# A second stage whose order is written out in 112 steps a period in place of 28

## The chip, the core and the metric

The kernel runs on one core of a Trainium2 chip. A core has five engines with a queue of their own each: TensorE (PE, with its weight loads, PEld), VectorE (DVE), ScalarE (ACT), GpSimd (POOL) and SyncE (SP, which here only issues DMAs). An engine works through its queue in order, and an instruction waits on semaphores for what other engines or DMAs have to deliver first. The metric is the device time of one execution in microseconds (us), as the median of several runs.

## The reference

Two layers, each behind a layer norm and added to its input. The first is a selective scan over 16 sequences of 1024 tokens with 512 channels and 16 states. The second keeps a part of the tokens (mixture of depths): a router scores every token, the 128 best of each sequence are found, and the best 127 of them go through attention and a feed-forward block; all the others pass through. Cut to the second layer:

```python
def _L0_ffn_ref(x, attention_mask, position_ids, router_w, ..., ln1, ln2):
    weights = (x @ router_w)[..., 0] + router_b[0]
    k = int(CAP * s)                       # 128 of 1024
    topv, topi = jax.lax.top_k(weights, k)
    thr = topv[:, -1]
    sel_mask = (weights > thr[:, None]).astype(x.dtype)
    sel_idx = jnp.sort(topi[:, :kc], axis=1)          # kc = 127
    x_sel = x[bidx, sel_idx]
    m_sel = m[bidx[:, :, None], sel_idx[:, :, None], sel_idx[:, None, :]]
    hn = rmsnorm(x_sel, ln1)
    q = rope(heads(hn @ wq), pos_sel); kk = rope(heads(hn @ wk), pos_sel); v = heads(hn @ wv)
    sc = jnp.einsum('bhqd,bhkd->bhqk', q, kk) / np.sqrt(hd) + m_sel[:, None]
    a = jax.nn.softmax(sc, axis=-1)
    o = (a @ v) @ wo
    x1 = x_sel + o
    x2 = x1 + jax.nn.gelu(rmsnorm(x1, ln2) @ w1) @ w2
    out = jnp.zeros_like(x).at[bidx, sel_idx].set(x2 * w_sel[..., None])
    return out + x * (1.0 - sel_mask)[..., None]
x = x + scan_layer(_layernorm(x))
x = x + _L0_ffn_ref(_layernorm(x), ...)
```

## The kernel before, in words

Everything is float32. `build` runs two stages one after the other. `scan_layer` computes the first layer and leaves its result in one DRAM tensor per sequence (`x1_dram`); the change does not touch it. `ffn_layer` is the second stage.

`ffn_layer` is a software pipeline over the 16 sequences. Its last lines run 18 periods, p = -1 to 16. In period p five generators run side by side, each on another sequence: `feed(p-1)` (the feed-forward block), `attention(p)`, `keep_others(p)` (the tokens that pass through), `select(p+1)` (top 128, gathers, first norm) and `scores(p+2)` (router). A period is a loop over `PERIOD` = 28 values of a clock. At each value the five are resumed once in that fixed sequence. A generator goes on issuing instructions until it meets an `until(k)` with k larger than the clock, and pauses there. So the numbers in `until(...)`, and nothing else, set the order in which the instructions of the five sequences stand in the engines' queues (`tc.manual_schedule()`: nothing is reordered later). They are no times. An engine that waits for one sequence's data also holds back what the other four put behind it.

What each generator does, with the lines that are spoken of later:

- `scores(b)` (L765, with `Router.scores` from L102): eight chunks of 128 tokens, each loaded as half of a tile `x1a`; per chunk on DVE `bn_stats` (L118), `bn_aggr` (L119) and a product with the router's weights (`xw`, L120). Then variance (ACT root, L128), the scores (`w_pad`, L139), a transpose on PE (`wt_ps`, L144), a copy on ACT (`w_t`, L146), and two DMAs on SP: `w_dram` (L148) and back, spread over all partitions, as `w_row` (L150). `w_row` is what `select` of the next period compares with.
- `select(b)` (L774): for each of eight chunks the rank of every token is counted on DVE (`junk` L788 and L792, `tie` L797), all ranks are added (L802, L803), eight one-hot tiles `sel` are made (L808), a threshold is summed (L815, L816). PE picks positions, weights and indices (`sd_ps`, L822; copy on ACT L826); DVE turns them into row numbers (`at`, L830 to L836); POOL gathers the mask's rows (`m_rows`, L838) and the tokens (`x1_sel`, L842). Then the angles (L861 to L868), the mask's transposes on PE (`tp_m`, L731) and their copies (`mT`, L874), `xs` (L877), the selected mask (`ms_ps`, L883), the first norm (`rmsnormed`), sine and cosine on ACT (`trig`, L891 and L892, then DVE L894), and the transposed, weighted norm `hnT` (L742).
- `attention(b)`: products with `wq`, `wk`, `wv` (L922), rotation of q and k on DVE (L934 to L942), transposes (`tp_q`, `tp_k`), logits (`sc`, L964), softmax: scaled and masked logits `a` (L970) and maximum `mx` (L976) on DVE, exponentials on ACT (L978), reciprocal `sm` (L987) and product (L988) on DVE; transposes of the weights (`tp_a`, L994; copies `aT`, L996), `o_ps` (L1003), `at_ps` (L1011), the residual on DVE (L1015), the second norm and `h2T` (L742).
- `feed(b)`: four `up` products of four matmuls each (L1029), GELU on ACT (L1034), transposes (`tp_g`), sixteen `ff_ps` matmuls (L1054), the residual and the weight on DVE (L1059, L1062), and on POOL a scatter that adds the rows to `out` (L1063).
- `keep_others(b)`: per pair of chunks two ACT instructions in place on a tile `x1b` (L908) and a store to `out` from SP (L912).

Matmul results go to PSUM banks: tag "mm" has four (`up`, the projections, `sc`, `at_ps`), "tp" two (all transposes, `sd_ps`, `ms_ps`), and `o` and `ff` one each. The loads of `x1a` and `x1b` (L673) are issued at fixed values of the clock. A logical float32 matmul of 512 columns appears as two records in the trace, a transpose as one.

Of the kernel before, what the change touches and what calls it, by code (L numbers as in the profile page):

```python
# [625 lines left out]
def ffn_layer(  # L626
# [8 lines left out]
    nc = tc.nc  # L635
# [10 lines left out]
    UP = F // 512  # L646
    PERIOD = 28
    assert K == P and RG * ND == H and UP == 4
# [112 lines left out]
    def scores(b):  # L761
        def chunk(c):
            if c == 2:
                load(b, 6, "x1a")
            return x1_of["x1a", b, c // 2 * 2][:, c % 2, :]  # L765

        first = 9 if b == 1 else 0
        return router.scores(
            b, until, [first + c if first or c < 6 else c + 7 for c in range(NT)] + [19, 20, 22],
            chunk, lambda c: row.tile([P, D], F32, tag="tmp", name=f"xw_{b}_{c}"),  # L770
            lambda name: pst.tile([P, 512], F32, tag="tp", name=name), True,
        )

    def select(b):  # L774
# [7 lines left out]
        for c in range(NT):  # L782
            yield from until(c)
            mine = w_col[:, c : c + 1]
            lo, hi = c * P, (c + 1) * P
            junk = row.tile([P, L], mybir.dt.bfloat16, tag="junk", bufs=1, name=f"junk_{b}_{c}")
            if c:
                nc.vector.tensor_scalar(  # L788
                    junk[:, :lo], w_row[:, :lo], mine, None, ALU.is_ge, ALU.add,
                    accum_out=cnt[:, 0, c : c + 1],  # L790
                )
            nc.vector.tensor_scalar(  # L792
                junk[:, lo:], w_row[:, lo:], mine, None, ALU.is_gt, ALU.add,
                accum_out=cnt[:, 1, c : c + 1],
            )
            tie = row.tile([P, P], F32, tag="tie", bufs=1, name=f"tie_{b}_{c}")
            nc.vector.scalar_tensor_tensor(  # L797
                tie, w_row[:, lo:hi], mine, earlier, ALU.is_equal, ALU.mult,
                accum_out=cnt[:, 2, c : c + 1],
            )  # L800
# [3 lines left out]

        yield from until(8)
        sel = keep.tile([P, NT, P], F32, tag="sel", bufs=1, name=f"sel_{b}")
# [11 lines left out]

        yield from until(10)
        sd_ps = pst.tile([P, 512], F32, tag="tp", name=f"sd_ps_{b}")  # L820
        for c in range(NT):
            nc.tensor.matmul(  # L822
                sd_ps[:, :SIDE], sel[:, c, :], side[:, c, :], start=(c == 0), stop=(c == NT - 1)
            )
        sd = small.tile([P, SIDE], F32, tag="sd", name=f"sd_{b}")
        nc.scalar.copy(sd, sd_ps[:, :SIDE])  # L826
        yield from until(12)
        at_f = small.tile([P, 3], F32, tag="at_f", name=f"at_f_{b}")
# [23 lines left out]
        keeping[b] = (by, plus)  # L852
        yield from until(15)

# [14 lines left out]

        yield from until(19)  # L870
        mT = row.tile([P, NT, P], F32, tag="mT", bufs=1, name=f"mT_{b}")
        for q in range(0, NT, 4):
            tp = turned(m_rows[:, q * P : (q + 4) * P], f"m_{b}_{q}")
            nc.scalar.copy(mT[:, q : q + 4, :], tp)  # L874
        yield from until(20)
        xs = keep.tile([P, D], F32, tag="xs", bufs=3, name=f"xs_{b}")
        nc.scalar.activation(  # L877
            xs, x1_sel, AF.Identity, bias=sd[:, OFF : OFF + 1], scale=sd[:, RSTD : RSTD + 1]
        )
        yield from until(20)  # L880
        ms_ps = pst.tile([P, 512], F32, tag="tp", name=f"ms_ps_{b}")
        for c in range(NT):
            nc.tensor.matmul(  # L883
                ms_ps[:, :P], mT[:, c, :], sel[:, c, :], start=(c == 0), stop=(c == NT - 1)
            )
        yield from until(21)
# [12 lines left out]
    def keep_others(b):  # L899

        by, plus = keeping.pop(b)
        for q in range(0, NT, 2):
            yield from until(1 + q if q < 6 else 18)
# [8 lines left out]
            nc.sync.dma_start(  # L912
                out[b, q * P : (q + 2) * P, :].rearrange("(c p) d -> p c d", p=P), x1
            )

    def attention(b):
        x1_sel, xs, sd, at, ms, trig, hnT = picked.pop(b)
        def projected(name, k):
            ps = psm.tile([P, D], F32, tag="mm", name=f"{name}_ps_{b}")
            for c in range(ND):  # L920
                yield from until(k + c // 2)
# [33 lines left out]
        yield from until(8)  # L955
        kT = taken(turned(k, f"k_{b}"), f"kT_{b}", "kT")
        a_of = []
        for g in range(0, RG, 2):
            yield from until(9 + g // 2)
            sc = [psm.tile([P, ND, P], F32, tag="mm", name=f"sc_{b}_{g + i}") for i in range(2)]  # L960
            for c in range(ND):
                for i in range(2):
# [21 lines left out]
        for g in range(RG):  # L984
            a, ak, sm = a_of[g]
            yield from until(11 + g)
            nc.vector.reciprocal(sm, sm)  # L987
            nc.vector.tensor_tensor(  # L988
                ak, ak, sm.unsqueeze(2).to_broadcast([P, ND, KC]), ALU.mult
            )  # L990
            yield from until(12 + g)
            tp = pst.tile([P, ND, P], F32, tag="tp", name=f"tp_a_{b}_{g}")
# [4 lines left out]
            aT.append(t)  # L997
        yield from until(16)
        o_ps = psa.tile([P, ND, P], F32, tag="o", name=f"o_ps_{b}")
# [9 lines left out]
        for c in range(ND):  # L1009
            yield from until(17 + c // 2)  # L1010
# [3 lines left out]
        yield from until(19)  # L1014
        nc.vector.tensor_tensor(xs, xs, at_ps, ALU.add)  # L1015
        h2 = rmsnormed(xs, f"h2_{b}")
        yield from until(23)
        h2T = gained(turned(h2, f"h2_{b}"), 1, f"h2T_{b}", "qT")
        attended[b] = (x1_sel, xs, sd, at, h2T)

    def feed(b):
# [3 lines left out]
        def unit(f):  # L1025
            up = psm.tile([P, 512], F32, tag="mm", name=f"up_{b}_{f}")
            for c in range(ND):
                yield from until(2 * f + c // 2)
                nc.tensor.matmul(  # L1029
# [4 lines left out]
            nc.scalar.activation(g, up, AF.Gelu_apprx_tanh)  # L1034
            yield from until(2 * f + 3)
            gT[f] = taken(turned(g, f"g_{b}_{f}"), f"gT_{b}_{f}", "gT", 4)
# [10 lines left out]
        todo = [(f, c) for f in range(UP) for c in range(4)]  # L1047
        plan = {9: 1, 11: 2, 13: 1, 14: 1, 15: 1, 16: 1, 17: 1, 19: 3, 20: 3, 21: 2}
        assert sum(plan.values()) == len(todo)
        for k in sorted(plan):  # L1050
            yield from until(k)
            for _ in range(plan[k]):
                f, c = todo.pop(0)
                nc.tensor.matmul(  # L1054
                    ff_ps, gT[f][:, c, :], w2_sb[:, f * 4 + c, :],
                    start=(f == 0 and c == 0), stop=(f == UP - 1 and c == 3),
                )
        yield from until(24)
        nc.vector.tensor_tensor(xs, xs, ff_ps, ALU.add)  # L1059
# [11 lines left out]
    with tc.manual_schedule():  # L1071
        for p in range(-1, B + 1):
# [89 lines left out]
```

## Time and profile before

| what | us |
|---|---|
| median of three runs (lowest, highest) | 3870.18 (3868.7, 3882.78) |
| the profiled execution: its own time | 3882.19 |
| its span, first to last instruction | 3880.5 |
| first `up` product of the second stage begins at | 2910.9 |
| mean distance of two periods' first `up`, over 13 periods (2910.9 to 3715.6) | 61.9 |
| busy within these 804.7: PE / DVE / ACT / POOL | 752.9 / 594.0 / 415.0 / 89.8 |
| the last two distances | 58.7, 56.5 |
| last first `up` (3830.9) to the end | 49.6 |

The granted TensorE clock is 0.95 on average over those 13 periods. Times in the timeline and in the chain of waits count from the span's start. The chain of waits is followed back from the last instruction: at each step to what released it, or to the instruction before it on the same engine. A row of it has a start, a length, an engine, a tile and a line.

### The profile page before, as it was taken

The page shows a single profiled execution, that of the slowest core. Times are in us where ns is not written, and L with a number is a line of the kernel's source. Part 1 is how long each engine was busy: PE and PEld are TensorE (multiplying, and loading weights), DVE is VectorE, ACT ScalarE, POOL GpSimd, SP SyncE. Part 2 cuts the span into 40 slices and gives each one's busy share as a digit, 9 for nine tenths or more (in the row PEclk, how much of TensorE's full clock was granted, in tenths as well). Part 3 has the DMA queues.
Part 4 walks back from the last instruction along what each step waited for, and adds up shares of the span by engine and source line. Part 5 has one row for each costly group of instructions (what it writes and reads, how often), then busy time and mean ns, then how long its engine had stood idle before and what let it go on. Part 6 is the DMA issues. An engine that isn't in the chain of part 4 may idle for free.

```text
span 3880.5 us, 89258 instructions
## 1 busy us (share of the span) xinstructions
PE 3562.9 (92%) x35365; PEld 2272.0 (59%) x35365; DVE 3444.8 (89%) x5145; ACT 3160.5 (81%) x5532; POOL 2718.1 (70%) x1452
## 2 busy tenths in 40 slices
PE   7999999999999999999999999999859999999997
PEld 4666666666666666666666666666434545445543
DVE  7999999999999999999999999999978686777751
ACT  8999999999999999999999999999534555555453
POOL 4999999999999999999999999999700101011110
PEclk9999999999999999999999999999969999999999
DMA  5343434434343343434343443434273443434331
GB/s 174 84 125 84 127 104 101 131 91 130 83 126 105 104 108 102 132 88 127 84 125 106 107 124 89 130 89 129 80 252 104 144 124 123 151 95 155 96 111 36
DMA packets 366508, 444.49 MB, mean 115 GB/s; under 512 B 181484, under 2 KB 251288, under 8 KB 361482
## 3 DMA queue, kind: packets, MB, share of 16 engines
q1 hardware_dynamic: 321928, 383.91, 32.6%
q0 software_dynamic: 39952, 50.54, 6.6%
q8 instruction: 279, 4.57, 0.5%
q10 hardware_dynamic: 4210, 4.33, 0.3%
q14 instruction: 139, 1.14, 0.1%
HBM read 361.36 MB, written 110.66 MB: 122 GB/s over the span
## 4 chain that ended last, share of the span: by engine, by line
PE 37%; ACT 32%; DVE 24%; issue 4%; DMA 3%; POOL 0%; POOLq 0%; DVEq 0%; ACTq 0%
ACT da L478 14%; PE db L490 10%; ACT v L470 8%; PE y L534 7%; DVE da L503 7%; PE db L492 5%; PE ff_ps L1054 4%; PE pp L312 3%; DVE junk L792 2%; DVE junk L788 2%; DVE r_st L118 2%; PE tpu L305 2%; PE at_ps L1011 1%; ACT delta L381 1%; DVE xw L120 1%
## 5 line engine op out<-in xcount | busy, mean ns | idle before, releaser
L515 POOL TENSOR_TENSOR hc<-da,ct 128x1024 f32<-128x1024 f32 x1024 | 2419.1, 2399 | 176.5 <-DVE da L503 160.2
L490 PEld LDWEIGHTS db<-dg,du 128*128 128x128 f32 x7168 | 978.0, 191 | 752.3 <-DVE da L503 562.7
L478 ACT ACTIVATE da<-delta,a_sb 128x512 f32<-128x512 f32 x2048 | 1409.1, 715 | 1.4 <-POOL carry L521 0.9
L490 PE MATMUL db<-dg,du 128*128 128x128 f32 x7168 | 1246.3, 291 | 130.7 <-DVE da L503 118.9
L503 DVE TENSOR_TENSOR_SCAN da<-da,carry,db 128x512 f32<-128x512 f32 x1024 | 1226.8, 1260 | 28.0 <-PE db L492 13.5
L503 DVE TENSOR_TENSOR_SCAN da<-da,db 128x512 f32<-128x512 f32 x1024 | 1171.0, 1199 | 25.3 <-PE db L492 23.9
L470 ACT ACTIVATE v<-du,bT 128x512 f32<-128x512 f32 x1152 | 825.1, 716 | 39.4 <-PE db L492 33.9
L492 PE MATMUL db<-ident,v 128*128 128x128 f32 x4608 | 841.4, 274 | 0.0
L534 PE MATMUL y<-hc,eye 32*32 32x512 f32 x16384 | 640.0, 606 | 2.9 <-POOL hc L515 2.9
L492 PEld LDWEIGHTS db<-ident,v 128*128 128x128 f32 x4608 | 575.5, 142 | 0.0
L817 POOL PARTITION_ALL_REDUCE thr<-thr_s x16 | 6.2, 384 | 439.5 <-DVE thr_s L816 439.5
L1063 POOL DMA_INDIRECT out<-xs,at x15 | 71.3, 4754 | 333.3 <-DVE trig L894 261.1
L1054 PE MATMUL ff_ps<-w_sb,gT 128*128 128x512 f32 x512 | 273.0, 652 | 0.0
L1029 PE MATMUL up<-w_sb,h2T 128*128 128x512 f32 x512 | 240.6, 598 | 4.0 <-DVE h2T L742 4.0
L534 PEld LDWEIGHTS y<-hc,eye 32*32 32x32 f32 x16384 | 143.3, 103 | 118.5 <-issue 77.9
L736 ACT COPY gT<-tp_g 128x512 f32<-128x512 f32 x64 | 38.2, 596 | 165.8 <-PE tp_g L731 165.8
L1029 PEld LDWEIGHTS up<-w_sb,h2T 128*128 128x128 f32 x512 | 92.7, 191 | 100.6 <-issue 92.7
L384 POOL TENSOR_TENSOR delta<-delta,rest 128x1024 f32<-128x1024 f32 x62 | 146.5, 2363 | 5.5 <-ACT delta L381 5.4
L978 ACT ACTIVATE a<-a,mx 128x127 f32<-128x127 f32 x256 | 98.8, 387 | 55.3 <-DVE mx L976 52.6
L792 DVE TENSOR_SCALAR_CACHE_REDUCE junk<-w_row,side 128x1024 bf16<-128x1024 f32 (+7 forms) x128 | 103.4, 808 | 37.3 <-DMA w_row<-w_dram 37.3
L344 PE MATMUL z<-xp,dt_sb 97*128 97x512 f32 x256 | 132.5, 599 | 2.0 <-DVE rest L349 1.9
L1054 PEld LDWEIGHTS ff_ps<-w_sb,gT 128*128 128x128 f32 x512 | 93.9, 206 | 64.7 <-issue 64.6
(210 smaller groups left out, 4013.0 us busy)
## 6 DMA issues: line engine op xcount, KB each, us to landing
ct<-bc SPq DMA_DIRECT2D x256, 512.0 KB, 4.2
dg<-field SPq DMA_DIRECT2D x384, 128.0 KB, 2.1
x<-in_x SPq DMA_DIRECT2D x16, 2048.0 KB, 14.0
x1b<-x SPq DMA_DIRECT2D x64, 512.0 KB, 3.8
out<-x1b SPq DMA_DIRECT2D x64, 512.0 KB, 5.8
xt<-in_x SPq DMA_DIRECT2D x31, 1024.0 KB, 7.9
x<-du POOLq DMA_DIRECT2D x31, 1024.0 KB, 8.5
x1a<-x SPq DMA_DIRECT2D x60, 512.0 KB, 5.0
```

What stands on the lines that cost most here:

```text
L344: nc.tensor.matmul(z, dt_sb[:, dc * P : (dc + 1) * P], xp, start=True, stop=True)
L384: nc.gpsimd.tensor_tensor(delta[:, dc : dc + 2, :], delta[:, dc : dc + 2, :], rest[:, dc : dc + 2, :], ALU.add)
L470: nc.scalar.activation(v_of[h, n][:, c - m, :], du[:, c, :], AF.Copy, scale=bT[:, c, n : n + 1])
L478: nc.scalar.activation(da_of[h, n][:, dc, :], live[h][1][:, dc, :], AF.Exp, scale=a_sb[:, dc, n : n + 1])
L490: nc.tensor.matmul(out, live[h][2][:, c, ch], dg[:, c, :], start=True, stop=True)
L492: nc.tensor.transpose(out, v[:, c - m, ch], ident)
L503: nc.vector.tensor_tensor_scan(da[:, dc, :], da[:, dc, :], db_of.pop(g), carry[b][:, dc, n : n + 1] if half else 0.0, ALU.mult, ALU.add,)
L515: nc.gpsimd.tensor_tensor(hc, da_of[h, n][:, dc - 1 : dc + 1, :], ct_of[h][:, n % G, :].unsqueeze(1).to_broadcast([P, 2, LH]), ALU.mult,)
L534: nc.tensor.matmul(ys[i][j * S : (j + 1) * S, :], weights(r, j), rows(r, j), start=start, stop=stop, tile_position=(i * S, j * S),)
L792: nc.vector.tensor_scalar(junk[:, lo:], w_row[:, lo:], mine, None, ALU.is_gt, ALU.add, accum_out=cnt[:, 1, c : c + 1],)
L1029: nc.tensor.matmul(up, h2T[:, c, :], w1_sb[:, c, f * 512 : (f + 1) * 512], start=(c == 0), stop=(c == ND - 1),)
L1054: nc.tensor.matmul(ff_ps, gT[f][:, c, :], w2_sb[:, f * 4 + c, :], start=(f == 0 and c == 0), stop=(f == UP - 1 and c == 3),)
```

## The change

Every `until(...)` of the second stage takes its number from one table, and a period has 112 steps; four new steps stand for one old. The loads that hung on the clock are at four times their old values. No instruction is added or taken away and no operand changes; only the order in the queues does. `Router.scores` is unchanged and gets its steps as before. The diff, cut to its core:

```diff
-    PERIOD = 28
+    PERIOD = 112
+
+    AT = {
+        "score": (0, 0, 5, 9, 9, 13, 49, 54, 66, 66, 80),
+        "score_1": (36, 40, 44, 48, 52, 56, 60, 64), "rank": (3, 11, 19, 23, 24, 25, 27, 27),
+        "one_hot": 22, "side": (37, 38, 38, 38, 38, 39, 39, 41), "side_out": 7, "rows": 52,
+        "angle": 69, "mask_T": (69, 77), "norm": 95, "mask": (75, 76, 81, 81, 82, 83, 83, 85),
+        "norm_1": 97, "trig": 109, "norm_T": 91, "others": (6, 10, 18, 68), "q": (1, 1, 14, 26),
+        "q_turn": 22, "k": (9, 9, 9, 19), "k_turn": 14, "v": (8, 19, 24, 25), "q_T": 0,
+        "k_T": 1, "logits": (36, 38), "soft": (35, 42, 42, 48), "a": (33, 33, 47, 50),
+        "a_T": (39, 39, 51, 59), "o": 64, "wo": (68, 69, 69, 71), "res": 67, "h_T": 81,
+        "up": (0, 0, 0, 0, 0, 0, 6, 6, 8, 6, 11, 11, 14, 17, 21, 19), "g_T": (14, 20, 27, 35),
+        "down": (39, 43, 43, 51, 55, 55, 64, 68, 72, 76, 76, 80, 80, 80, 84, 89), "end": 102,
+    }
@@ scores
-        first = 9 if b == 1 else 0
+        at = AT["score"]
         return router.scores(
-            b, until, [first + c if first or c < 6 else c + 7 for c in range(NT)] + [19, 20, 22],
+            b, until, AT["score_1"] + at[NT:] if b == 1 else at,
@@ select
         for c in range(NT):
-            yield from until(c)
+            yield from until(AT["rank"][c])
...
-        yield from until(8)
+        yield from until(AT["one_hot"])
...
-        yield from until(10)
+        yield from until(AT["side"][0])
         sd_ps = pst.tile([P, 512], F32, tag="tp", name=f"sd_ps_{b}")
         for c in range(NT):
+            yield from until(AT["side"][c])
             nc.tensor.matmul(
...
+        yield from until(AT["side_out"])
...
-        yield from until(12)
+        yield from until(AT["rows"])
...
-        yield from until(19)
+        yield from until(AT["mask_T"][0])
...
-        yield from until(20)
+        yield from until(AT["norm"])
...
-        yield from until(25)
+        yield from until(AT["trig"])
         nc.scalar.activation(trig[:, 0, :], turn, AF.Sin)
         nc.scalar.activation(trig[:, 1, :], ang, AF.Sin)
-        yield from until(26)
         nc.vector.tensor_scalar(trig[:, 2, :], trig[:, 1, :], -1.0, None, ALU.mult)
-        yield from until(24)
+        yield from until(AT["norm_T"])
         hnT = gained(turned(hn, f"hn_{b}"), 0, f"hnT_{b}", "hnT")
@@ attention
-        q_ps = yield from projected("wq", 1)
-        yield from until(3)
+        q_ps = yield from projected("wq", AT["q"])
+        yield from until(AT["q_turn"])
         q = rotate("wq", q_ps)
-        k_ps = yield from projected("wk", 3)
-        yield from until(5)
+        k_ps = yield from projected("wk", AT["k"])
+        yield from until(AT["k_turn"])
         k = rotate("wk", k_ps)
-        v_ps = yield from projected("wv", 5)
-        yield from until(7)
+        v_ps = yield from projected("wv", AT["v"])
+        v = taken(v_ps, f"v_{b}", "v")
+        yield from until(AT["q_T"])
         qT = taken(turned(q, f"q_{b}"), f"qT_{b}", "qT")
-        v = taken(v_ps, f"v_{b}", "v")
...
             for i in range(2):
+                yield from until(AT["soft"][g + i])
                 a = late.tile([P, ND, P], F32, tag="a", bufs=4, name=f"a_{b}_{g + i}")
@@ feed
-        plan = {9: 1, 11: 2, 13: 1, 14: 1, 15: 1, 16: 1, 17: 1, 19: 3, 20: 3, 21: 2}
-        for k in sorted(plan):
+        for k in AT["down"]:
             yield from until(k)
...
-        yield from until(24)
+        yield from until(AT["end"])
@@ the loop over a period
-                if p == 0 and 1 <= k <= ND + NF // ND:
-                    load_heavy(k - 1)
-                if k in (12, 14, 18):
-                    load(p + 3, (12, 14, 18).index(k) * 2, "x1a")
-                if k in (13, 15, 21):
-                    load(p + 1, (13, 15, 21).index(k) * 2, "x1b")
+                if p == 0 and k % 4 == 0 and 1 <= k // 4 <= ND + NF // ND:
+                    load_heavy(k // 4 - 1)
+                if k in (48, 56, 72):
+                    load(p + 3, (48, 56, 72).index(k) * 2, "x1a")
+                if k in (52, 60, 84):
+                    load(p + 1, (52, 60, 84).index(k) * 2, "x1b")
```

A step that is smaller than one that the same generator has already passed takes effect at once (`until` returns when the clock is there). So within `attention` the transposes of q and k (steps 0 and 1) come directly behind the last `wv` matmul (step 25), and the rotation of k (14) directly behind that of q (22).

The order of one period that results on the two engines that the prediction walks along (names as above; a number in brackets is how many logical matmuls or which group):

```
PE before: up(4) wq(2) up(2) wq(2) tp_g up(2) wk(2) up(2) wk(2) tp_g up(2) wv(2) up(2) wv(2) tp_g
  up(2) tp_q tp_k tp_g ff(1) sc(16) sd(8) ff(2) tp_a ff(1) tp_a ff(1) tp_a ff(1) tp_a ff(1)
  o ff(1) at(4) ff(3) tp_m(8) ff(3) ms(8) ff(2) wt tp_h tp_hn
PE after: up(6) wq(2) up(6) tp_g up(1) wq(1) up(1) tp_g up(2) wq(1) wk(4) wv(4) tp_q tp_k
  tp_g tp_g sc(8) sd(5) ff(1) sd(3) sc(8) ff(2) tp_a tp_a ff(1) tp_a ff(2) tp_a ff(1)
  o ff(1) at(3) tp_m(4) at(1) ff(3) tp_m(4) ff(3) wt tp_h ff(2) ms(8) tp_hn
DVE before: hnT rank0 chunk0 rank1 chunk1 rank2 chunk2 turn_q rank3 chunk3 rank4 chunk4 turn_k
  rank5 chunk5 rank6 rank7 sel thr 4x(a mx) a0 a1 at a2 chunk6 a3 chunk7 angles
  xs(+at) norm2 scores norm1 h2T xs(+ff) L894
DVE after: hnT chunk0 chunk1 rank0 chunk2 chunk3 chunk4 rank1 chunk5 rank2 rank3 rank4 rank5
  turn_q turn_k rank6 rank7 sel thr 4x(a mx) a0 a1 a2 chunk6 a3 at chunk7 scores angles
  xs(+at) norm2 h2T norm1 xs(+ff) L894
```

Here chunk is L118 to L120, rank L788 to L797, turn a rotation, 4x(a mx) L970 and L976, a0 to a3 L987 and L988, at L830 to L836.

More of the change, by code (lines that the diff above doesn't have):

```diff
@@ L852, in select @@
         keeping[b] = (by, plus)
-        yield from until(15)
+        yield from until(AT["angle"])
         if b == 0:
@@ L868, in select @@
         nc.vector.tensor_scalar(turn, turn, -1.0, math.pi / 2, ALU.mult, ALU.add)
-        yield from until(19)
+        yield from until(AT["mask_T"][0])
         mT = row.tile([P, NT, P], F32, tag="mT", bufs=1, name=f"mT_{b}")
         for q in range(0, NT, 4):
+            yield from until(AT["mask_T"][q // 4])
             tp = turned(m_rows[:, q * P : (q + 4) * P], f"m_{b}_{q}")
             nc.scalar.copy(mT[:, q : q + 4, :], tp)
-        yield from until(20)
+        yield from until(AT["norm"])
         xs = keep.tile([P, D], F32, tag="xs", bufs=3, name=f"xs_{b}")
@@ L879, in select @@
         )
-        yield from until(20)
+        yield from until(AT["mask"][0])
         ms_ps = pst.tile([P, 512], F32, tag="tp", name=f"ms_ps_{b}")
         for c in range(NT):
+            yield from until(AT["mask"][c])
             nc.tensor.matmul(
@@ L885, in select @@
             )
-        yield from until(21)
+        yield from until(AT["norm_1"])
         hn = rmsnormed(xs, f"hn_{b}")
@@ L902, in keep_others @@
         for q in range(0, NT, 2):
-            yield from until(1 + q if q < 6 else 18)
+            yield from until(AT["others"][q // 2])
             if q == 2:
@@ L917, in attention, with projected @@
         x1_sel, xs, sd, at, ms, trig, hnT = picked.pop(b)
-        def projected(name, k):
+        def projected(name, at):
             ps = psm.tile([P, D], F32, tag="mm", name=f"{name}_ps_{b}")
             for c in range(ND):
-                yield from until(k + c // 2)
+                yield from until(at[c])
                 nc.tensor.matmul(
@@ L943, in rotate @@
             return t.rearrange("p h s f -> p (h s f)")
-        q_ps = yield from projected("wq", 1)
-        yield from until(3)
+        q_ps = yield from projected("wq", AT["q"])
+        yield from until(AT["q_turn"])
         q = rotate("wq", q_ps)
-        k_ps = yield from projected("wk", 3)
-        yield from until(5)
+        k_ps = yield from projected("wk", AT["k"])
+        yield from until(AT["k_turn"])
         k = rotate("wk", k_ps)
-        v_ps = yield from projected("wv", 5)
-        yield from until(7)
+        v_ps = yield from projected("wv", AT["v"])
+        v = taken(v_ps, f"v_{b}", "v")
+        yield from until(AT["q_T"])
         qT = taken(turned(q, f"q_{b}"), f"qT_{b}", "qT")
-        v = taken(v_ps, f"v_{b}", "v")
-        yield from until(8)
+        yield from until(AT["k_T"])
         kT = taken(turned(k, f"k_{b}"), f"kT_{b}", "kT")
@@ L958, in attention @@
         for g in range(0, RG, 2):
-            yield from until(9 + g // 2)
+            yield from until(AT["logits"][g // 2])
             sc = [psm.tile([P, ND, P], F32, tag="mm", name=f"sc_{b}_{g + i}") for i in range(2)]
@@ L985, in attention @@
             a, ak, sm = a_of[g]
-            yield from until(11 + g)
+            yield from until(AT["a"][g])
             nc.vector.reciprocal(sm, sm)
@@ L990, in attention @@
             )
-            yield from until(12 + g)
+            yield from until(AT["a_T"][g])
             tp = pst.tile([P, ND, P], F32, tag="tp", name=f"tp_a_{b}_{g}")
@@ L997, in attention @@
             aT.append(t)
-        yield from until(16)
+        yield from until(AT["o"])
         o_ps = psa.tile([P, ND, P], F32, tag="o", name=f"o_ps_{b}")
@@ L1009, in attention @@
         for c in range(ND):
-            yield from until(17 + c // 2)
+            yield from until(AT["wo"][c])
             nc.tensor.matmul(
@@ L1013, in attention @@
             )
-        yield from until(19)
+        yield from until(AT["res"])
         nc.vector.tensor_tensor(xs, xs, at_ps, ALU.add)
         h2 = rmsnormed(xs, f"h2_{b}")
-        yield from until(23)
+        yield from until(AT["h_T"])
         h2T = gained(turned(h2, f"h2_{b}"), 1, f"h2T_{b}", "qT")
@@ L1027, in unit @@
             for c in range(ND):
-                yield from until(2 * f + c // 2)
+                yield from until(AT["up"][4 * f + c])
                 nc.tensor.matmul(
@@ L1034, in unit @@
             nc.scalar.activation(g, up, AF.Gelu_apprx_tanh)
-            yield from until(2 * f + 3)
+            yield from until(AT["g_T"][f])
             gT[f] = taken(turned(g, f"g_{b}_{f}"), f"gT_{b}_{f}", "gT", 4)
@@ L1047, in feed @@
         todo = [(f, c) for f in range(UP) for c in range(4)]
-        plan = {9: 1, 11: 2, 13: 1, 14: 1, 15: 1, 16: 1, 17: 1, 19: 3, 20: 3, 21: 2}
-        assert sum(plan.values()) == len(todo)
-        for k in sorted(plan):
+        for k in AT["down"]:
             yield from until(k)
[L1052 to L1057, printed above, removed]
-        yield from until(24)
+            f, c = todo.pop(0)
+            nc.tensor.matmul(
+                ff_ps, gT[f][:, c, :], w2_sb[:, f * 4 + c, :],
+                start=(f == 0 and c == 0), stop=(f == UP - 1 and c == 3),
+            )
+        yield from until(AT["end"])
         nc.vector.tensor_tensor(xs, xs, ff_ps, ALU.add)
```

## The prediction

> **What bounds the kernel now.** I first read the busy shares by slice: the scan fills the first 2800 us with every engine near its limit and is not touched. The second stage is a chain of periods: 13 distances of 61.9 us in a row, with PE busy for 752.9 of 804.7 us, which looks like a bound by PE. The chain of waits over one steady period (start, length, piece) says something else.
>
> ```profile
> 3094.95 0.12 PE wt_ps L144
> ...
> 3095.10 0.27 ACT w_t L146
> ...
> 3095.38 1.20 DMA w_dram<-w_t
> ...
> 3096.59 3.73 DMA w_row<-w_dram
> ...
> 3100.43 1.29 DVE junk L792 x2
> 3101.72 0.27 DVE tie L797 x2
> 3101.99 0.62 DVE r_st L118
> ...
> 3133.47 0.69 DVE a L988
> ...
> 3134.30 0.68 PE tp_a L994 x4
> ...
> 3156.89 0.12 PE wt_ps L144
> ...
> 3157.03 0.27 ACT w_t L146
> ```
>
> It is a closed loop: from `wt_ps` to the next `wt_ps` 61.94 us. Three legs make it up: the scores' way through DRAM, 3094.95 to 3100.43, 5.48 us; DVE without a pause, 3100.43 to 3134.30, 33.87 us; PE, 3134.30 to 3156.89, 22.59 us. Anything shortened outside this loop is worth nothing. The table of waits (engine, what it waited for, total us, times, longest) from 2900 to 3740 has the two joints of the loop:
>
> ```profile
> DVE junk L792 <- DMA w_row<-w_dram: 32.7, 14, 2.5
> PE tp_a L994 <- DVE sm L987: 40.2, 13, 4.2
> ```
>
> DVE idles up to 2.5 us for `w_row`, PE up to 4.2 us for the first softmax weights. The third view is busy time in three stretches of that period (stretch, length, busy time and count of PE, PEld, DVE, ACT, POOL, then granted clock, DMA share, GB/s):
>
> ```profile
> 3128.20:3131.40 3.20, 3.20 (x6) 0.91 (x5) 3.10 (x6) 2.02 (x11) 0.38 (x1) 0.58 0.71 204
> 3131.40:3134.30 2.90, 0.04 (x1) 0.03 (x1) 2.73 (x7) 2.75 (x16) 0.00 (x0) 0.88 1.03 393
> 3134.30:3138.70 4.40, 4.40 (x12) 2.35 (x13) 3.22 (x14) 2.71 (x11) 1.16 (x2) 0.64 0.81 262
> ```
>
> The clock is near half before PE's pause and again behind it. The second time lies in the PE leg and is paid.
>
> **The change, leg by leg.** Nothing is added or removed, so each price below is a row of before put into another place. Times count from the start of a period's first `up`, which follows `tp_hn` at once.
>
> *The scores' way.* `wt_ps` now stands before `tp_h`, two `ff`, `ms` and `tp_hn`: 0.43 + 1.72 + 1.78 + 0.43 = 4.36 us of PE (a group of four transposes 0.43, a logical 512-column matmul 0.86, `ms` 1.78, all at full clock from this period's chain). `w_row` lands 5.48 us behind `wt_ps`, so at 1.0. The first rank that reads it comes behind `hnT` and two score chunks on DVE, at 2.3 + 2 x 1.41 = 5.1 (chunk: 3101.99 to 3103.40). The 5.48 leaves the loop, with 4.1 us to spare; if the landing were that much later, it would be back.
>
> *What takes its place.* DVE now starts behind `hnT`, and `hnT` stands behind L894, which waits for the sines. They follow `ms_ps` on ACT: copy 0.27, table load 1.28, two sines 0.42; then L894 0.17 and `hnT` 0.68: 2.82, less the 0.43 that `tp_hn` takes on PE meanwhile, 2.4. Neighbouring instructions overlap by some 0.1, so I take 2.3 behind the end of `tp_hn`.
>
> *DVE leg.* From `hnT` to the first weighted softmax group stand the same six chunks, eight ranks, two rotations, `sel`, threshold, four `a`/`mx` pairs and one L987/L988 as in the 33.87 us of before: 33.9. Is its input there? `wq` is done by PE at 16 x 0.86 + 4 x 0.86 + 2 x 0.43 = 18.1; DVE comes to it at 2.3 + 8.5 + 9.6 = 20.4 (six chunks, six ranks of 1.6). `wk` is done at 21.5, asked for at 22.4. So the earlier up, k and v products cost nothing and gain nothing by themselves: DVE hides them, with 0.9 us left at the tightest; uncovered, each us late is a us a period. The logits' second group is written by 31.6 and read at 32.6. Exponentials (about 1.55 a group on ACT) are done by 32.9, 34.4, 36.0, 37.6, before DVE asks.
>
> *PE leg.* PE reaches `tp_a` at 33.3 and DVE delivers at 36.2, so the pause stays, at 2.9. From there to the end of `tp_hn`: `tp_a` 4 x 0.43, thirteen `ff` 11.18, `o` 1.01, `at` 3.43, `tp_m` 0.87, `wt` 0.12, `tp_h` 0.43, `ms` 1.78, `tp_hn` 0.43: 20.97. Before, the same pieces without `wt`, `tp_h` and `tp_hn` make 19.99, and the leg took 22.59: 2.6 went to the low clock and to groups whose weights came late on DVE behind row numbers and a chunk. Now the second `tp_a` follows the first at once and waits 0.81 - 0.43 = 0.4. A new wait comes with `tp_m`, half of which stands before the last `at` matmul:
>
> ```profile
> L838 POOL DMA_INDIRECT m_rows<-in_mask,at x12: 1005/1023/1527, 3013.0 to 3694.6; - x12
> DMA to landing us min/median/max: 5.2/6.4/7.1
> ```
>
> Row numbers are ready 4.3 behind the first weighted group (two more groups 0.81 each, a chunk 1.41, a group 0.81, the numbers 0.47), at 40.5; POOL issues 0.8 later (3136.45 to 3137.23 before), landing at 47.7. PE is there at 36.2 + 1.72 + 0.4 + 4.3 + 1.01 + 2.58 = 46.2 and waits 1.5 (0.3 to 2.2 over the landing's range); the last `at` and all behind it wait too. Before, `tp_m` came 12.7 us after that issue. A low-clock window between the two uses up the same wait, so I put 1.5 for both: a window is some 3.4 us (the stretches above) and costs 1.7. No row shows it under the new order; the bounds are 0 and two windows, 3.4.
>
> The Trainium skill (TensorE: Matmul & The Clock Gate, "HAM oscillation — how this bites in real kernels") asks for no PE pauses above about 3.4 us. By that rule a pause of 2.9 leaves the clock full, the upper bound drops to the gather's 2.2, and the rival of no change loses its chance. The trace does not bear it out: the clock stood at 0.58 before a pause of 2.90, behind thin `sc` and `sd` matmuls.
>
> *Other queues.* The scatter still follows DVE's last two `xs` instructions, ahead of L894 in both orders, and POOL is busy for only 89.8 of 804.7. SP's stores hang on it:
>
> ```profile
> SPq L912 <- DMA out<-xs,at: 337.6, 12, 29.4
> ```
>
> It blocks SP until some 26 us into a period in both orders; what stands behind (loads wanted at 49 of 112 steps or in the next period) has the rest of the period, and the load of `x1a`'s last pair now stands before the blocked store. ACT is busy for 415.0 of 804.7 and covers the moved pass-through work; if not, a late `gT` or `hn` would stop PE (closest: `hn` for `tp_hn`, about 0.6 us).
>
> *Sum of a period:* 2.3 + 33.9 + 21.0 + 0.4 + 1.5 = 59.1, against 61.9: 2.8 gained, 13 times, 36.4. Bounds: 2.3 + 33.9 + 21.0 + 0.4 + 0.3 = 57.9 (gain 4.0) and 2.3 + 33.9 + 21.0 + 0.4 + 3.4 = 61.0 (gain 0.9).
>
> *Start and end.* In the first full period nothing covers the scores' way:
>
> ```profile
> 2850.24 1.28 DVE L792 TENSOR_SCALAR_CACHE_REDUCE junk<-w_row,side 128x1024 bf16<-128x1024 f32 x1 [4.66 <-DMA w_row<-w_dram]
> ```
>
> Chunks fill these 4.7 us; bounds 0 and 7 (plus one period's gain). The last two distances, 58.7 and 56.5, have no chunks (8.5 us less DVE), so only PE's pauses can shrink: 1 us, bounds 0 and 2. The last 49.6 us hang on two scatters in a row (27.2 us for one), unchanged. Total 36.4 + 4.7 + 1 = 42.1. The profiled execution, 3882.19 (span 3880.5), would take 3840.1. It lies 12.0 above the median of the runs, so the predicted median is 3870.2 - 42.1 = 3828.
>
> **The rivals.**
>
> *The clock takes it.* With the same pause of 2.9 and thin matmuls around it, two or more windows at half clock fall into the PE leg: 61.0 a period or a little more, 3858 to 3870. For it: before lost 2.6 there. Against: part of that was late weights, which the new order removes. Chance 0.09.
>
> *Slower: the gather becomes the joint.* `tp_m` is in PE's queue before `at`'s last matmul, so each us by which `m_rows` lands later than 6.4 + 2.8 = 9.2 us after issue makes the kernel slower by 13. At 12 us: 13 x 2.8 = 36 more, less some 5 from the ends: about 3901. For it: DMA engines stood at 1.03 and 393 GB/s in the stretch just before the gather. Against: twelve landings of 5.2 to 7.1, in that very neighbourhood; and SP's burst, let go at about 26, is 15 us old at the new issue (41.3) where it was 12.3 before. Chance 0.06.
>
> *Faster still.* The clock stays up and the gather is quick: 57.9 a period, 3809. For it: `sd` is split by a wide `ff`. Chance 0.13.
>
> That the change does nothing is excluded where it counts: `wt_ps` stands 4.36 us of PE earlier and two chunks come before the first rank.
>
> **How the numbers follow.** Forecast 0.72, rivals as above. A measurement of this kernel tells about 0.5% (19 us) from no change. Below 3851: forecast nearly whole, and the last rival: 0.84. Within: 0.10. Above 3890: 0.06. Range 3807 to 3852: from the quick case to just inside the clock's.
>
> **What would show it.** Distances of first `up` near 59; no wait of `junk` for `w_row`; a wait of PE's `tp_m` for `m_rows` of some 1 us; DVE unbroken from `hnT` to the first `tp_a`; PE still waiting near 2.9 there. Wrong it is if DVE shows pauses between `hnT` and `mx`, if `tp_m` waits above 4 us, or if the clock's low windows reach three a period.

## The result and the profile after

The changed kernel takes 3828.36 us (median of four runs, 3825.81 to 3839.21), the kernel before 3875.32 in the same rounds (3868.7 to 3882.78): ratio 0.9882, 95% interval 0.9863 to 0.9901. The forecast was 3828, range 3807 to 3852. The profiled execution took 3825.81 with a span of 3824.1.

The mean distance of two periods' first `up`, over the same 13 periods, is 59.09 us in place of 61.9 (forecast 59.1). It is much the sharper measure here: the scan, which no run touches, ends at 2787.8 to 2820.1 in the profiles of this case (its last instruction on DVE), 32 us apart, so totals within some 10 us of each other tell little.

First rows of the table of waits of the kernel after, from 2900 to 3662, which is its 13 periods but for the first 6 us (engine, what it waited for, total us, times, longest):

```profile
DVE trig L910 <- ACT trig L909: 28.9, 12, 2.4
PE tp_a L1011 <- DVE sm L1004: 15.9, 11, 2.0
PE at_ps L1028 <- ACT oT L749: 3.9, 9, 0.5
PE tp_g L744 <- ACT qT L749: 3.8, 13, 0.3
DVE a L987 <- PE sc L980: 1.2, 3, 0.5
PE tp_m L744 <- DMA m_rows<-in_mask,at: 0.2, 1, 0.2
```

`w_row` is gone from it: 32.7 us before, nothing now. In its place stands the wait for the sines (L894 of the kernel before is L910 here). PE's wait for the softmax has fallen from 40.2 to 15.9, and the gather hardly shows. The wait of `at_ps` for `oT` is in the profile of this kernel alone; no run of the list below has it, though e2, e3, e5, e7 and e11 keep the order on PE around it, and why it came here is open. The chain of waits over one period (start, length, piece):

```profile
3188.57 0.27 ACT ms L906
...
3188.84 1.28 ACT L908
...
3190.13 0.21 ACT trig L908
3190.34 0.12 ACT trig L909
...
3190.48 1.31 DVE trig L910
...
3194.07 1.20 DVE junk L805 x2
...
3225.02 0.69 DVE a L1005
3225.85 0.68 PE tp_a L1011 x4
...
3234.60 2.58 PE at_ps L1028 x6
...
3246.33 1.80 PE ms_ps L900 x16
3248.42 1.28 ACT L908
```

It is the loop that the prediction drew: the copy of `ms`, the sines' table load (1.28) and the two sines on ACT, L910 on DVE (its record of 1.31 overlaps `hnT` and the chunk behind it), DVE without a break to the weighted softmax, PE from `tp_a` to `ms_ps`, and the table load again. No DMA is in it. PE's timeline in another period (start, length, instruction, in brackets the idle time before it and what ended it) shows the joints:

```profile
3101.91 1.16 PE L980 MATMUL sc<-kT,qT 32*128 32x127 f32 x16
3103.00 1.98 PE L1068 MATMUL ff_ps<-w_sb,gT 128*128 128x512 f32 x4
3106.99 1.49 PE L1011 MATMUL tp_a<-ident,a 128*127 128x128 f32 x8 [2.01 <-DVE sm L1004]
...
3115.39 2.84 PE L1028 MATMUL at_ps<-wo_sb,oT 128*128 128x512 f32 x6 [0.49 <-ACT oT L749]
3118.45 0.63 PE L744 MATMUL tp_m<-ident,m_rows 128*128 128x128 f32 x4 [0.21 <-DMA m_rows<-in_mask,at]
```

Where the time came from, between the two profiled executions (spans 3880.5 and 3824.1): 36.5 from 13 periods of 2.81 each, 2.5 from the last two distances (57.7 and 55.0), 5.9 from the start of the second stage, and 11.2 from the scan, whose last instruction on DVE ended at 2795.5 in place of 2806.7. The change does not touch the scan, so those 11.2 are the spread of executions; without them 45 are left, which agrees with the medians' 47.

### The profile page after: what moved, and what is told of

Same layout as the page of the kernel before. It is cut to its first block, busy times and chain, and to the rows that moved or that the text cites. A ratio compares the mean times of both kernels' runs of the same rounds, so it can differ in the third digit from the quotient of the medians.

```text
span 3824.1 us, 89195 instructions
## 1 busy us (share of the span) xinstructions
PE 3547.3 (93%) x35365; PEld 2271.5 (59%) x35365; DVE 3434.7 (90%) x5145; ACT 3161.8 (83%) x5532; POOL 2715.1 (71%) x1452
## 3 DMA queue, kind: packets, MB, share of 16 engines
q8 instruction: 279, 4.57, 0.5%
## 4 chain that ended last, share of the span: by engine, by line
PE 43%; ACT 30%; DVE 21%; issue 4%; DMA 1%; POOL 0%; POOLq 0%; DVEq 0%; SPq 0%; ACTq 0%
ACT da L478 13%; PE db L490 10%; DVE da L503 9%; PE y L534 8%; ACT v L470 7%; PE db L492 5%; PE ff_ps L1068 5%; PE pp L312 3%; PE up L1046 3%; PE tpu L305 2%; PE at_ps L1028 1%; DVE junk L805 1%; ACT delta L381 1%; ACT u L296 1%; ACT w L352 1%
## 5 line engine op out<-in xcount | busy, mean ns | idle before, releaser
L830 POOL PARTITION_ALL_REDUCE thr<-thr_s x16 | 6.2, 384 | 434.0 <-DVE thr_s L829 434.0
L1068 PE MATMUL ff_ps<-w_sb,gT 128*128 128x512 f32 x512 | 260.8, 631 | 0.0
L1046 PE MATMUL up<-w_sb,h2T 128*128 128x512 f32 x512 | 232.6, 592 | 0.0
L1051 ACT ACTIVATE g<-up 128x512 f32<-128x512 f32 x64 | 38.2, 597 | 117.9 <-PE up L1046 106.5
L853 POOL DMA_INDIRECT m_rows<-in_mask,at x16 | 16.3, 1016 | 165.9 <-issue 98.3
L312 PE MATMUL pp<-uT,xp_sb 128*96 128x512 f32 x256 | 130.3, 592 | 0.7 <-ACT uT L307 0.7
```

Source lines behind the costliest of these rows:

```text
L312: nc.tensor.matmul(pp[:E, :], xp_sb[:, dc, :], uT[:, dc, :], start=(dc == 0), stop=(dc == ND - 1))
L1046: nc.tensor.matmul(up, h2T[:, c, :], w1_sb[:, c, f * 512 : (f + 1) * 512], start=(c == 0), stop=(c == ND - 1),)
L1068: nc.tensor.matmul(ff_ps, gT[f][:, c, :], w2_sb[:, f * 4 + c, :], start=(f == 0 and c == 0), stop=(f == UP - 1 and c == 3),)
```

## The experiments

Means over 13 periods of each profile, in us from a period's first `up`; "low" is the time a period with the clock granted at half speed; the ratio is to the kernel before in the same rounds, with its interval. Each kernel has one profile, and its low time is that of one execution.

| run | period | hnT ends | first rank | first tp_a | PE's pause there | tp_m waits | low | median | ratio |
|---|---|---|---|---|---|---|---|---|---|
| before | 61.90 | 1.67 | 4.02 | 37.89 | 3.09 | 0 | 5.99 | | |
| after | 59.09 | 2.46 | 5.16 | 36.35 | 1.23 | 0 | 3.15 | 3828.4 | 0.9882 (0.9863-0.9901) |
| e1 | 59.74 | 1.66 | 4.39 | 35.83 | 1.33 | 0 | 4.20 | 3835.9 | 0.990 (0.9872-0.9928) |
| e2 | 58.83 | 2.46 | 2.56 | 36.47 | 1.20 | 0.2 | 2.89 | 3837.4 | 0.9899 (0.9881-0.9917) |
| e3 | 59.23 | 2.06 | 4.77 | 36.42 | 0.85 | 0 | 4.46 | 3834.6 | 0.9881 (0.9859-0.9904) |
| e4 | 62.11 | 2.06 | 4.57 | 39.67 | 0.18 | 0 | 7.61 | 3873.3 | 0.9985 (0.9966-1.0005) |
| e5 | 58.76 | 0.89 | 3.63 | 36.23 | 1.28 | 0.3 | 2.63 | 3825.1 | 0.987 (0.9827-0.9912) |
| e6 | 58.52 | 2.46 | 5.16 | 36.27 | 1.72 | 0.2 | 1.31 | 3828.9 | 0.988 (0.9836-0.9923) |
| e7 | 59.07 | 2.46 | 5.16 | 36.42 | 1.29 | 0.2 | 3.41 | 3828.9 | 0.987 (0.9829-0.9912) |
| e8 | 58.20 | 0.90 | 3.63 | 36.18 | 1.72 | 0 | 1.12 | 3809.5 | 0.9821 (0.978-0.9862) |
| e9 | 58.62 | 0.89 | 3.63 | 36.50 | 1.49 | 0.1 | 2.36 | 3827.3 | 0.9861 (0.9832-0.9891) |
| e10 | 58.68 | 0.89 | 3.63 | 36.53 | 1.44 | 0.1 | 2.63 | 3839.9 | 0.9885 (0.9854-0.9917) |
| e11 | 58.42 | 2.46 | 5.16 | 36.47 | 1.53 | 0.1 | 1.61 | 3836.0 | 0.9881 (0.9849-0.9913) |
| e12 | 57.57 | 0.90 | 3.63 | 34.99 | 1.23 | 0.7 | 0.31 | 3802.8 | 0.9813 (0.979-0.9837) |

### Is it the scores' way through DRAM?

The change takes `w_row` off the loop in two ways at once: `wt_ps` stands 4.36 us of PE earlier, and two chunks cover the landing. e1 is the kernel before with nothing but the ranks moved behind chunks:

```diff
-            yield from until(c)
+            yield from until((2, 2, 3, 3, 4, 5, 6, 7)[c])
```

> The kernel before with one edit: the ranks of a period wait until two score chunks stand on DVE. Theory (the loop through w_row set the period): the wait of the first rank for w_row goes, the loop becomes hnT 1.7 + DVE 33.9 + PE leg 24.0 = 59.6 in place of 61.9, so 13 x 2.3 = 30 faster plus 3 to 5 at the start: about 3840. Rival (the new order on PE and the finer softmax did it: fewer stretches at low clock, shorter pauses): a period of 61.5 or more, 3865 to 3875.

The period fell to 59.74: this one line alone gives 2.2 of the change's 2.8 us. Is it the clock, since the low time fell too (5.99 to 4.20)? No: in e1 the one period without any low time took 59.74, eight with 3.41 us of it 59.67 to 59.96, four with 6.83 us 59.67 to 59.74; in the kernel before, four with 3.41 us took 61.6 to 61.9 and the others, with up to 10.2, 61.1 to 62.7.

The other 0.65 us lie between e1 and the kernel after: there `hnT` ends 0.80 later, the DVE leg (from there to the first `tp_a`) is 0.29 shorter and the PE leg (from the first `tp_a` to the next `up`) 1.16 shorter, 22.75 for 23.91. In e1 as before the fourth `tp_a` comes no sooner than 41.8, since on DVE `a3` stands behind `at` and chunk 6; the new order puts `at` behind `a3`. This is read from the rows; no run undid it alone.

e2 to e4 go the other way, from the kernel after: e2 puts the first rank ahead of the chunks again, e3 puts `wt_ps` back to the period's end, e4 does both.

```diff
-        "score": (0, 0, 5, 9, 9, 13, 49, 54, 66, 66, 80),
+        "score": (0, 0, 5, 9, 9, 13, 49, 54, 66, 66, 98),
-        "rank": (3, 11, 19, 23, 24, 25, 27, 27),
+        "rank": (0, 11, 19, 23, 24, 25, 27, 27),
```

> The changed kernel with the first rank back ahead of the first two score chunks. Theory: w_row lands about 1.5 after the period's first up, before hnT is there (2.5), so nothing waits: a period of 59.1, 0 to 1 us more at the start, no change against the changed kernel (3828). If chunks before ranks were needed, the first rank would show a wait of 1 us or more and the period would grow by it.

> The changed kernel with wt_ps back behind ms_ps, directly ahead of tp_hn. Theory: w_row then lands 5.48 - 0.55 = 4.9 after the first up; the first rank comes at 5.2, behind two chunks: no wait. The copy w_t now stands before the sines on ACT (0.27), so 59.1 to 59.4 a period, 3828 to 3833. If the early wt_ps alone made the gain, the period goes back towards 61.9 (3865).

> The changed kernel with both edits of E2 and E3 undone; all the rest of the new order stays. Theory: the first rank waits for w_row until 4.9 where hnT is done at 2.5 to 2.7, so the loop through w_row is back: 5.48 + 33.9 + 22.2 = 61.6 a period, 13 x 2.5 = 33 slower than the changed kernel, about 3861 to 3866. Rival (order on PE did it): 59.1 to 59.5, 3828 to 3834.

Each edit by itself costs nothing that this tells from the spread (58.83 and 59.23; the medians lie 6 to 9 us above that of the kernel after, which the periods do not show); with both, the period is 62.11 and the gain is gone in full, though all the rest of the new order is still there. DVE's timeline in e4 shows the old joint back, first in the period:

```profile
3089.76 0.32 DVE L910 TENSOR_SCALAR trig<-trig 128x16 f32<-128x16 f32 x1 [2.65 <-ACT trig L909]
3089.84 0.68 DVE L755 TENSOR_TENSOR hnT<-tp_hn,gain 128x512 f32<-128x512 f32 x1
3090.48 0.08 DVE L794 MEMSET cnt<- 128x24 f32 x1
3093.02 1.28 DVE L805 TENSOR_SCALAR_CACHE_REDUCE junk<-w_row,side 128x1024 bf16<-128x1024 f32 x1 [2.46 <-DMA w_row<-w_dram]
```

After `hnT` DVE stands for 2.46 us, and the first rank comes 2.0 later than in e2 (4.57 for 2.56). Not all of e4's loss is this wait. Its two periods with one low window took 60.6 and 60.8, the five with three windows 62.7 to 63.5: with PE slow ahead of `tp_a` (6.74 us a period at half clock there), DVE also waited 14.9 us in 12 periods for the logits, and `tp_k` waited 15.4 us in 13 periods for the rotated k, which is not in the list of the kernel after. So some 2 us a period of e4's loss are the loop, and the rest goes with the low clock; that the loop brought on the low clock is not shown. With e1's 2.2 the old loop is shown as the cause of most of the gain, and either cure alone is enough.

### Do the products' order and the gather matter?

e6 gives `up`, q, k and v their old steps in the kernel after:

```diff
-  "q": (1, 1, 14, 26), "q_turn": 22, "k": (9, 9, 9, 19), "k_turn": 14, "v": (8, 19, 24, 25),
-  "q_T": 0, "k_T": 1, "up": (0, 0, 0, 0, 0, 0, 6, 6, 8, 6, 11, 11, 14, 17, 21, 19), "g_T": (14, 20, 27, 35),
+  "q": (4, 4, 8, 8), "q_turn": 12, "k": (12, 12, 16, 16), "k_turn": 20, "v": (20, 20, 24, 24),
+  "q_T": 28, "k_T": 32, "up": (0, 0, 4, 4, 8, 8, 12, 12, 16, 16, 20, 20, 24, 24, 28, 28), "g_T": (12, 20, 28, 36),
```

> The kernel after, with the up, q, k and v products, both rotations, the transposes of q and k and those of g at four times their old steps (up and projections alternate again). Theory (the order of these products earns nothing by itself, DVE's queue hides it): period 59.1 within 0.4, DVE leg 33.9, total 3823 to 3834. Rival (up first, k and v sooner are part of the gain): the logits come later for DVE, the DVE leg grows by 0.5 us or more and the period is 59.6 to 61.9, total 3835 to 3866.

The DVE leg is 33.81 (33.89 after), and the period is not longer but 0.6 shorter, with less low clock (1.31 against 3.15) and without the wait of `at_ps` (0.3 a period after); the medians are the same. "Up products first" earned nothing. e7 computes the gather's row numbers one chunk later (`"rows": 55` for 52):

> The kernel after, with the row numbers of the gather computed behind chunk 7 in place of ahead of it (step 55 for 52), so POOL issues the mask's gather 1.41 us later; DVE's sum is the same. Theory (the gather has no slack to speak of: tp_m waited 0.2 in one period of 13, and PE's leg lies in the loop): tp_m waits for m_rows 0.5 to 1.6 us in most periods, period 59.6 to 60.4, total 3835 to 3845. Rival (the gather is covered by an us or more, or what PE loses there it has to spare): period 59.1, no wait above 0.3, total 3828.

The period, 59.07, is the rival's, but not its "no wait above 0.3". The row of e7:

```profile
PE tp_m L744 <- DMA m_rows<-in_mask,at: 2.9, 8, 1.1
```

Landing was quicker than in the profile of before: over these periods 4.3/5.3/6.5 us (least, median, most) in the kernel after, where the prediction took 6.4 from 5.2/6.4/7.1, and 4.1/4.5/5.7 in e7. In the kernel after the rows lie there 1.1 us on average before PE asks for them (from 0.1 too late to 2.7 early), in e7 0.15 (0.9 too late to 1.3 early). So the later issue used up the slack, and 8 periods of 13 began to wait; e7's four periods without low time took 58.2 to 59.2, the longer the more `tp_m` waited. The mean hides it, since the wait of `at_ps` of the kernel after (3.9 us in all) is not in e7.

### What sets the 59.1, and is there a better order?

By the chain, the wait for the sines comes first. e5 moves the instruction that needs them out of DVE's way:

```diff
         nc.scalar.activation(trig[:, 1, :], ang, AF.Sin)
-        nc.vector.tensor_scalar(trig[:, 2, :], trig[:, 1, :], -1.0, None, ALU.mult)
@@ attention
+        nc.vector.tensor_scalar(trig[:, 2, :], trig[:, 1, :], -1.0, None, ALU.mult)
         q = rotate("wq", q_ps)
```

> The kernel after, with one DVE instruction moved: the negation of the sine (L910) stands in attention just before the rotation of q, so hnT no longer waits for the sines. Theory (DVE's leg from hnT to the first tp_a is what sets the period, and PE has a pause of 1.23 us there on average): hnT ends 0.8 to 0.9 us behind the first up in place of 2.46, tp_a could come 1.6 us sooner; PE is there 2.0 us ahead in the periods at full clock and 0.0 to 0.6 ahead in those with a window at low clock, so the period becomes 59.1 - 1.0 = 58.1 (57.5 at full clock), pause 0.3, and the total falls by some 13, to about 3815. Rival (PE's own work and its clock set the period, the wait for the sines is hidden): period 59.1, total 3828, pause unchanged at 1.2.

`hnT` ended 1.57 sooner as expected, but the first `tp_a` only 0.12 sooner: a miss. DVE's leg grew to 35.34, since it now came too early for PE's products: it waited for `wk` 7.3 us in all (13 times, up to 0.6), for the logits 6.8 (13 times, up to 0.9). The 0.9 us of slack that the prediction put at `wk` was real, and it ended here. e8 adds to e5 a second `ff` between `o` and `at`:

```diff
-        "wo": (68, 69, 69, 71),  "mask_T": (69, 77),
+        "wo": (72, 73, 73, 75),  "mask_T": (73, 77),
```

> The kernel of the run before last but one in this list (negation of the sine in attention), and also a second ff matmul between o and at (wo at steps 72, 73, 73, 75; the first four transposes of the mask at 73), taken from the three ff that follow at. Theory: the wait of at_ps for oT (3.9 us in 9 periods, 0.5 each) goes, tp_m comes 0.86 us later behind the gather's issue, and the period is 57.6 to 57.8, total about 3809 to 3813. Rival (the clock takes it, as thin matmuls and PE's pauses stay): as without the ff, 58.1, total 3815; or the later at delays h2T for tp_h and the period is longer, 58.5.

The period fell to 58.20 and the median to 3809.5. The forecast total was met; the period's mean was not as short as expected, for the reason seen in e5, though the periods without low time took 57.8 to 58.2. But the wait of `at_ps`, which the edit was to remove, was not in e5 either, so it explains none of the 0.56 against e5. What fell is the wait of `tp_m` for the gather (3.4 us in 6 periods of e5, 0.2 in all in e8), which the later `tp_m` covers, and the low time (2.63 to 1.12 a period). e9 adds e6's product order (k turned at 24, v at 24, 24, 25, 25), and e10 sets the second logits group to step 36.

> The kernel of e8 (sine and ff moved), and the up, q, k and v products alternate again as in e6, the rotation of k at step 24. Theory (in e5 and e8 DVE began its leg 1.57 us sooner and lost nearly all of it to waits for wk, 0.6, and for the logits, 0.5, because the slack of 0.9 that the up-first order leaves was used up): with wk some 5 us sooner the wait of the rotation for wk goes, the DVE leg falls from 35.3 to 34.0 to 34.5, the first tp_a comes at 35.0 to 35.4, and the period at full clock is 56.8 to 57.2, its mean 57.0 to 57.6, the total 3796 to 3804. Rival (the products' order hides in any case, the leg of e5 and e8 is longer for another reason, as row loads or the rank's data): leg 35.3, period 58.2, total 3809.

> The kernel of e9, and the second group of logits right behind the first (step 36 for 38), ahead of the sd matmuls and the ff among them, so it is written 1.9 us sooner. Theory: the wait of the softmax's first DVE instruction for sc (0.5 a period in e8) goes, DVE leg 33.9 to 34.0, period at full clock 56.4 to 56.8, total 3790 to 3797. Rival (32 thin logits matmuls and sd in one stretch bring the clock down before tp_a, and PE, which is then only 0.5 us ahead of DVE, is late): windows at low clock in most periods, period 57.5 or more, total 3800 or more.

Both missed. The wait for `wk` is gone from e9, but the same time is lost at the next joint, as DVE's timeline shows:

```profile
2982.51 0.68 DVE L993 TENSOR_REDUCE mx<-a 128x4 f32<-128x508 f32 x1
2984.22 0.69 DVE L987 SCALAR_TENSOR_TENSOR a<-sc,ms 128x508 f32<-128x508 f32 x1 [1.03 <-PE sc L980]
```

DVE waits 1.03 us for the second logits group. e10's edit changed no order there: the second group comes only after the generator has passed the softmax's second step, 42. It is thus e9 run again (over the 13 periods every engine has the same instructions in the same order), and shows the scatter: 58.62 and 58.68 a period, but medians of 3827.3 and 3839.9 on one chip. e12 moves that step too:

```diff
-        "logits": (36, 38), "soft": (35, 42, 42, 48),
+        "logits": (36, 36), "soft": (35, 36, 42, 48),
```

> The kernel of e9, and the second group of logits truly right behind the first: logits at steps 36 and 36, softmax steps 35, 36, 42, 48 (in e10 the softmax's second step, 42, still held the second group behind sd and ff, so e10's order is that of e9). Theory (in e8, e9 and e10 the joint is PE's second group of logits to DVE: DVE waits 1.0 for it in every period at full clock, which keeps the first tp_a at 36.1): the wait goes, the first tp_a comes at 35.0 to 35.2, PE's pause falls from 1.85 to 0.8 to 1.0, the period at full clock is 56.7 to 56.9 in place of 57.8, and the total falls by some 13, to 3810 to 3820 beside e9's 3827, or lower where few windows at low clock fall into it. Rival (something else fixes tp_a at 36.1, as the exponentials on ACT, which are then only just done): the wait moves to sm, tp_a at 35.7 to 36.1, period at full clock 57.4 to 57.8.

The first `tp_a` came at 34.99, 1.51 sooner than in e9 (at full clock 34.96 for 36.08, 1.12 sooner), PE's pause was 1.36 in a period at full clock, and the fastest periods took 56.6 and 56.7. The forecast 56.7 to 56.9 for a period at full clock was met only in the one in which PE did not wait for the gather (56.65); the other ten took 57.0 to 58.8. The waits of e12 over its periods (the same columns as above):

```profile
PE tp_a L1011 <- DVE sm L1004: 16.2, 12, 1.4
PE tp_m L744 <- DMA m_rows<-in_mask,at: 9.5, 10, 2.0
```

Now PE does wait for the gather, 0.7 a period; landing there was 4.4/7.0/8.3. e12 is the fastest of the study, 3802.8, and its interval lies wholly below that of the kernel after; the two were not timed against each other on one chip.

### Do thin matmuls bring the clock down?

e11 is the kernel after with all `sd` matmuls in one stretch (`"side"` at 37 throughout):

> The kernel after, with all eight sd matmuls at step 37, so sc, sd and sc stand in one stretch of some 4.3 us of thin matmuls, and the wide ff that split it comes behind. Theory (the clock falls behind long stretches of thin matmuls): a window at low clock ahead of the first tp_a in 10 or more of the 13 periods (6 of 13 after), PE's pause there shrinks to 0.3 to 0.8, and the period grows by 0 to 0.3 only, since the pause of 2.0 takes it up: 59.1 to 59.4, total 3828 to 3833. Rival (the windows do not come from the thin matmuls): 4 to 8 of 13, pause 1.2, total 3828.

A miss for the theory: 3 of 13 periods had low clock before `tp_a`, fewer than the 6 of the kernel after, and the period was 58.42. A longer stretch did not add any window here; the last section shows why this run is a weak test.

## Why the prediction was right

*What bounds the kernel.* The closed loop through `w_row` is confirmed by e4 (loop back, gain gone) and e1 (loop opened by one line, most of the gain there).

*The scores' way.* The first rank began at 5.16 (forecast 5.1) without a wait. That 5.48 leaves the loop held; of the "4.1 us to spare" e2 shows 2.6, for there the first rank stands at 2.56 and waits for `w_row` in one period of 13 (0.4).

*What takes its place.* `hnT` ended at 2.46 (2.3).

*DVE leg.* 33.89 (33.9). "Costs nothing and gains nothing by themselves" is confirmed by e6, and the slack of 0.9 at `wk` by e5.

*PE leg.* From the first `tp_a` to the next `up` 22.75 (21.0 + 0.4 + 1.5 = 22.9), but by parts that stand otherwise. The 1.5 for gather and clock was over-sized: `tp_m` waited 0.2 in one period of 13, and 1.26 us a period at half clock in this leg cost half of that, 0.6. The 21.0 + 0.4 was under-sized: the three periods wholly at full clock took 22.39, 22.48 and 22.85 there, of which 0.44 to 0.52 is a wait that the prediction did not list (`at_ps` for `oT`, 3.9 us in 13 periods) and in the last 0.21 `tp_m`; the remaining 21.95 to 22.15 is 0.55 to 0.75 above the sum (0.3 to 0.6 in e6 and e11, whose full-clock periods without either wait took 21.7 to 22.0 there). The errors nearly cancel, and that is luck.

*The pause.* "So the pause stays, at 2.9" is the step that failed. It was 1.23. At full clock PE reached `tp_a` at 34.2, not 33.3, for the sum up to there was 0.9 short, 0.3 of it the wait of `tp_g` for the copy of qT in every period, which leaves 2.0; and 1.89 us a period at half clock ahead of `tp_a` took up to half their length from it. The period hardly felt it, because DVE sets that end: `tp_a` came 0.6 late in the two periods with 5.5 us of low time there, and 0.2 late in two others. The signs "a wait of `tp_m` of some 1 us" and "still waiting near 2.9" did not come, then; the others did, but for 1.2 us that DVE waited for the logits in three periods.

*Start and end.* 5.9 for 4.7, inside its bounds; 2.5 for 1, above its bound of 2: PE's pauses in the last two distances shrank by 3.0 in all, from 3.39 and 4.61 to 2.27 and 2.75. 42.1 in sum became 36.5 + 5.9 + 2.5 = 44.9, and the medians differ by 47.0. That 3828 was met to within 1 us is luck: the kernel before took 3875.3 beside it, where the prediction subtracts from 3870.2.

*The rivals.* The clock took less than two windows (period 59.09, not 61.0); nothing was slower. "The gather becomes the joint" did not come in this kernel, but e12 shows its mechanism once DVE is 1.4 us sooner, and e7 its beginning. "Faster still", 57.9 a period, was not the mean, but its size was right: the periods of e6 and e11 without low time and without a wait for the gather took 57.9 to 58.2, with the sines and the `ff` where the change puts them.

## What to carry to other kernels

Read the loop, not the busy shares: PE was busy for 94% of the stage, yet most of the gain came from moving one engine's first use of a slow round trip behind work that was there anyway. When a joint is removed, list the next slack on every engine with its number: here 0.9 at `wk`, then 1.0 at the logits, then the gather; an `hnT` 1.57 sooner brought the first `tp_a` only 0.1 sooner until the products and the logits were moved too. A step table with generators has two traps: a step smaller than one already passed takes effect at once, and a step that stands behind a larger one in the same generator does nothing (e10).

## What the runs showed of the clock

In all 14 profiles the half-clock windows of the 13 periods last 3.41 us or a whole multiple of it, and in each of the 13 with more than one window they start on one grid of 3.413 us, to within 0.001. Cutting PE's records along that grid, a stretch at full clock in which PE was busy for less than 45% was followed by a window at half clock in 44 of 46 cases; at 45 to 48% in 1 of 17; at 48 to 60% in none of 45. That is not the whole of it: these 44 are fewer than half of the 114 stretches at full clock that half clock followed, and 62 of the 114 were stretches in which PE was busy for over 80%. Busy time of three such stretches of the kernel after (stretch, length, busy time and count of PE, PEld, DVE, ACT, POOL, granted clock, DMA share, GB/s):

```profile
3042.18:3045.59 3.41, 3.23 (x22) 1.78 (x22) 3.34 (x6) 3.09 (x17) 0.00 (x0) 1.00 0.55 112
3045.59:3049.00 3.41, 1.45 (x9) 1.26 (x10) 3.21 (x9) 3.32 (x19) 0.00 (x0) 0.99 1.05 413
3049.00:3052.41 3.41, 3.41 (x8) 1.81 (x7) 3.24 (x15) 1.54 (x4) 0.12 (x1) 0.51 1.01 329
```

In the second, PE is busy for 1.45 of 3.41 (42%); in the third the clock is 0.51. So a pause of about 1.9 us (55% of 3.413) is enough when it falls wholly within one stretch of the grid: 2.0 in the kernel after lies above that, 1.85 in e8 at the border (1.12 us low a period), 1.36 in e12 below it (0.31). The Trainium skill (TensorE: Matmul & The Clock Gate, "HAM oscillation — how this bites in real kernels") speaks of pauses above about 3.4 us; these traces show low windows behind pauses of 2.0, so here the measurement decides. Stretches full of `sc` and `sd`, with wide matmuls and transposes in less than a fifth of them, were followed by half clock in 13 of 16 cases, with 30 to 40% in 42 of 130, with 40 to 50% in none of 35. That fits thin matmuls counting for less; e11 did not bear it out, and it stays open. e11 tests it weakly, for what a period does depends on where it falls on the grid: its last nine periods took 57.9 to 58.2, nearly seventeen stretches of 3.413 (58.03), so the thin matmuls stood within 0.6 us of one place of the grid in all nine, and no window came. In e1 a period of 59.74 is 17.5 stretches, and in its last nine periods the low time alternates between 3.41 and 6.83 us. So a number of windows from one profile says little on the order that was run.
